# Float32 projections as four products of 32 columns each, in a decoder layer on one core

## The chip, the core and the metric

The kernel runs on one core of a Trainium2 chip. The metric is the time of one execution on the device in microseconds. The core has five engines with their own instruction streams: TensorE (PE in the profile, its weight loads PEld), VectorE (DVE), ScalarE (ACT), GpSimd (POOL) and SyncE (SP, which here only issues DMAs). TensorE is an array of 128 rows by 128 columns. The rows carry the contraction, the columns the output partitions. A product (a matmul instruction of the kernel) first loads its stationary operand into the array and then streams its moving operand past it; results go to PSUM, which the kernel uses in banks of 128 partitions by 512 float32. A product that is less than 128 rows tall or less than 128 columns wide takes only a strip of the array, and products on different strips can run side by side.

## What is computed

One decoder layer on `x` of 128 sequences by 128 tokens by 256 features, in float32: self attention, cross attention with a context of the same shape, and a feed-forward block with ternary weights, each with a layer norm ahead of it and a residual sum behind it. Cut to what matters here:

```python
def attention(q_in, kv_in, Wq, Wk, Wv, Wo, mask):       # 16 heads of 16 features
    Q, K, V = q_in @ Wq.T + bq, kv_in @ Wk.T + bk, kv_in @ Wv.T + bv
    scores = einsum("bhqd,bhkd->bhqk", Q, K) / 4         # cross: where(mask == 0, 1e-9, scores)
    return einsum("bhqk,bhkd->bhqd", softmax(scores), V) @ Wo.T + bo
x = x + attention(layernorm(x), layernorm(x), ...)       # self
x = x + attention(layernorm(x), context, ..., mask)      # cross
h = layernorm(gelu(layernorm(x) @ ternary(W_fc).T)) * ln_w + ln_b
x = x + h @ ternary(W_proj).T
```

The eight products with `Wq`, `Wk`, `Wv` and `Wo` (four for each attention, all of 256 by 256 weights) are the projections that the change is about.

## The kernel before

**Tiling.** Work goes by groups of four sequences, 512 tokens, so there are 32 groups. Features lie on partitions in two chunks of 128 (`CC = 2`). A weight matrix is one tile `[128, 2, 256]` in float32.

**Streams and order.** The kernel is written as Python generators, one for each kind of work, and each `yield` ends a step. Stream A is the attention itself (`maxima`, `outputs`, `transposed_scores`, `transposed_maxima`, `weights`, one sequence at a time), n prepares self attention (`prepare_self`), k the keys and values of cross attention (`prepare_keys`), c ends self attention and makes the queries of cross attention (`prepare_cross`), f ends cross attention and does the feed-forward block (`finish`). Three strings of letters, `START`, `ORDER` (112 letters, run 28 times) and `END`, say which stream does its next step. Each engine executes its instructions in exactly that order, so on TensorE a projection step can stand behind a step of any other stream.

**The projections.** `product_halves` makes the transposed queries and keys (tiles `pq`, `pk`, line 317): for one half `o` of the output features it issues two products, one for each chunk `c` of the contraction, with a stationary block of 128 by 128 weights and a moving operand of 512 tokens. There is a step border between the two. `row_halves` makes values and output rows (`pv`, `po`, line 329): for two blocks of 128 tokens it issues two products each, with the 128 tokens stationary and 256 weight columns moving. All of them are products of the whole array, in float32. ScalarE takes `pq` and `pk` out of PSUM (lines 374 and 351), VectorE `pv` and `po` (lines 365 and 411).

**Shapes on TensorE.** In the profile a group's shape gives rows*columns of the array. Beside the projections these are there:

- whole array, 128*128: transposes `pt` (line 297), `pg` (470) and `pn` (718), and the feed-forward products `ph` (436) and `py` (494), these two with float32r operands;
- row strips, 32*128, four side by side: the scores `s` (691), the transposed scores `st` (749) and what is added to them (773);
- column strips, 128*32, four side by side: the attention outputs `av` (794), written as four products into partitions 0 to 31, 32 to 63, 64 to 95 and 96 to 127 of one bank;
- 32*32, sixteen side by side: the mask products (680), in bfloat16.

A float32 product leaves two LDWEIGHTS and two MATMUL records in the trace; a transpose or a float32r product leaves one of each.

**Banks.** `bank(name)` gives one of three PSUM banks to each step of projections, transposes and feed-forward in turn (`BANKS = 3`); scores have two pairs of banks of their own, `av` and `pn` share one.

Of the kernel before, what the change touches and what calls it, by code (L numbers as in the profile page):

```python
# [27 lines left out]
P = 128  # L28
# [3 lines left out]
CC = D // P  # L32
# [5 lines left out]
S4 = 4  # L38
# [31 lines left out]
def tile_decoder_layer(ctx: ExitStack, tc: tile.TileContext, a: dict, out: bass.AP):  # L70
    nc = tc.nc
# [115 lines left out]
    def bank(name):  # L187
        return ps_mm.tile([P, 512], F32, name=name, tag="mm")
# [113 lines left out]
    def transposed_copy(x):  # L302
# [7 lines left out]
        yield from transposed(x, evacuate)  # L310
        return xn_t[0]

    def product_halves(w, o, src_t, name):

        out = bank(name)
        for c in range(CC):
            nc.tensor.matmul(  # L317
                out, w[:, c, o * P : (o + 1) * P], src_t[:, c], start=(c == 0), stop=(c == CC - 1)
            )
            if c == 0:  # L320
                yield
        return out

    def row_halves(w, src_t, j0, name):

        rows = bank(name).rearrange("p (j d) -> p j d", j=2)
        for j in range(2):
            for c in range(CC):
                nc.tensor.matmul(  # L329
                    rows[:, j],  # L330
                    src_t[:, c, (j0 + j) * P : (j0 + j + 1) * P],
                    w[:, c],
                    start=(c == 0),
                    stop=(c == CC - 1),
                )
            if j == 0:
                yield
        return rows
# [3 lines left out]
    def keys_values(w, src_t, unit):  # L342
        nonlocal n_values


        for o in range(CC):
            pk = yield from product_halves(w["k"], o, src_t, "pk")
            if o == 0:
                kt = unit["k"] = p_act.tile([P, CC, 2, T], F32, name="kt", tag="kt", bufs=3)
            for e in range(2):  # L350
                nc.scalar.activation(
                    kt[:, o, e],
                    pk,
                    AF.Identity,
                    bias=w["bk"][:, o, e : e + 1],
                    scale=parity[:, e : e + 1],
                )
            yield
        for j0 in range(0, G, 2):
            rows = yield from row_halves(w["v"], src_t, j0, "pv")  # L360
            if j0 == 0:
                v = unit["v"] = values[n_values % 3]
                n_values += 1
            heads = v[:, j0 : j0 + 2, 0 : H * VC].rearrange("p j (h d) -> p j h d", d=VC)
            nc.vector.tensor_copy(heads[:, :, :, 0:HD], rows.rearrange("p j (h d) -> p j h d", d=HD))  # L365
            if j0 == 0:
                yield

    def queries(w, xn_t, unit):
        for o in range(CC):  # L370
            pq = yield from product_halves(w["q"], o, xn_t, "pq")
            if o == 0:
                qt = unit["q"] = p_act.tile([P, CC, T], F32, name="qt", tag="qt", bufs=3)
            nc.scalar.activation(qt[:, o], pq, AF.Identity, bias=w["bq"][:, o : o + 1], scale=Q_SCALE)
            if o == 0:
                yield
# [15 lines left out]
    def projected(w, x, sums, o_raw):  # L392

        r = p_stat.tile([P, T // 8], F32, name="r", tag="r", bufs=2)
        nc.vector.reciprocal(r, sums)

        by_head = p_dram.tile([CC, 8, T], F32, name="by_head", tag="by_head")
        nc.sync.dma_start(by_head.rearrange("o h (j t) -> (o h j) t", j=8), r)
        factors = p_act.tile([P, CC, T], F32, name="factors", tag="factors", bufs=1)
        for o in range(CC):  # L400
            nc.sync.dma_start(factors[:, o], by_head[o][:, None, :].to_broadcast([8, HD, T]))
        yield

        for o in range(CC):
            for half in range(2):
                tok = slice(half * T // 2, (half + 1) * T // 2)
                nc.gpsimd.tensor_tensor(o_raw[:, o, tok], o_raw[:, o, tok], factors[:, o, tok], ALU.mult)  # L407
        yield
        for j0 in range(0, G, 2):
            rows = yield from row_halves(w["o"], o_raw, j0, "po")  # L410
            nc.vector.tensor_tensor(x[:, j0 : j0 + 2], x[:, j0 : j0 + 2], rows, ALU.add)
            yield
# [481 lines left out]
```

## Time and profile before

| | us |
|---|---|
| median of 3 runs | 2746.52 (2745.23 to 2748.5) |
| the profiled execution, its own time | 2749.66 |
| its span, first to last instruction | 2747.6 |
| LDWEIGHTS busy | 1953.2 (71%) |
| VectorE busy | 2051.7 (75%) |
| ScalarE busy | 1552.0 (56%) |
| GpSimd busy | 1367.6 (50%) |

TensorE's costliest groups, by line and shape. The columns are the line, engine and operation, output and inputs, rows*columns of the array, the moving operand, the number of records, their busy time (us) with what overlaps counted once, the mean time of one (ns), and the idle time ahead of them.

```profile
L691 PE MATMUL s<-kt,qt 32*128 32x256 f32 x4096 | 296.9, 401 | 1.6 <-ACT w_t L782 1.5
L794 PE MATMUL av<-w_t,v 128*32 128x128 f32 x8192 | 278.1, 276 | 4.4 <-DVE q_max L723 1.3
...
L329 PE MATMUL pv<-xattn_wv,ctx_t 128*128 128x256 f32 x512 | 134.4, 386 | 0.0
L317 PE MATMUL pk<-ctx_t,xattn_wk 128*128 128x512 f32 x256 | 134.1, 607 | 0.0
```

The mean time of one record is longer than the room it takes: [...] the next ones start meanwhile. Busy time divided by count is nearer to the room. The granted TensorE clock is 0.995 of full speed over the span. The DMA engines are busy about a fifth of the time.

### The profile page before, as it was taken

What the parts mean: (1) busy time and instruction counts of PE and PEld (TensorE: products, weight loads), DVE (VectorE), ACT (ScalarE), POOL (GpSimd) and SP (SyncE); (2) the same over time, 40 slices, a digit from 0 to 9 for tenths busy, and PEclk for the clock granted to TensorE, in tenths of its full rate; (3) what the DMA queues carried; (4) which work ended last, traced back from release to release, by engine and by line L of the source; (5) the groups of instructions that cost most, each with busy time, mean ns of one, the idle gap of its engine ahead of it and who ended that gap; (6) DMA issues with size and microseconds to landing.
All of it is one profiled execution on the core that took longest, in us unless ns stands there. A gap on an engine that the chain in (4) does not pass through costs nothing.

```text
span 2747.6 us, 76951 instructions
## 1 busy us (share of the span) xinstructions
PE 2698.6 (98%) x32845; PEld 1953.2 (71%) x32845; DVE 2051.7 (75%) x3793; ACT 1552.0 (56%) x2380; POOL 1367.6 (50%) x1427
## 2 busy tenths in 40 slices
PE   7999999999999999999999999999999999999998
PEld 4567777777777777777777777777777777777767
DVE  5777777777787777787777877777877777877677
ACT  3355565555655555655555655555665556655446
POOL 2355454545554545544554545454545455545334
PEclk9999999999999999999999999999999999999999
DMA  3121121221211211212211212211212212212210
GB/s 102 49 50 32 51 50 41 57 51 34 55 42 49 57 43 40 57 41 50 57 34 48 57 36 54 57 34 49 50 40 57 57 30 53 45 46 50 49 25 16
DMA packets 110044, 130.28 MB, mean 47 GB/s; under 512 B 32264, under 2 KB 69000, under 8 KB 109704
## 3 DMA queue, kind: packets, MB, share of 16 engines
q1 hardware_dynamic: 109704, 125.37, 19.0%
q8 instruction: 260, 4.26, 0.6%
q14 instruction: 80, 0.66, 0.1%
HBM read 71.38 MB, written 18.84 MB: 33 GB/s over the span
## 4 chain that ended last, share of the span: by engine, by line
PE 94%; DVE 3%; POOL 1%; issue 1%; ACT 1%; DMA 1%; SPq 0%; ACTq 0%; DVEq 0%; POOLq 0%
PE st L749 10%; PE s L691 10%; PE av L794 9%; PE py L494 9%; PE ph L436 9%; PE po L329 9%; PE pq L317 8%; PE pv L329 8%; PE pk L317 8%; PE pg L470 4%; PE pt L297 3%; PE st L773 3%; PE s L680 2%; PE pn L718 1%; DVE mx L702 1%
## 5 line engine op out<-in xcount | busy, mean ns | idle before, releaser
L702 DVE TENSOR_REDUCE mx<-s 128x8 f32<-128x1024 f32 x512 | 600.6, 1215 | 66.5 <-PE s L691 64.3
L782 ACT ACTIVATE w_t<-st 128x1024 f32<-128x1024 f32 x512 | 496.7, 1023 | 194.2 <-PE st L749 166.3
L274 POOL TENSOR_SCALAR rstd<-agg 128x4 f32<-128x4 f32 (+2 forms) x163 | 40.0, 246 | 1099.8 <-DVE agg L269 1094.3
L279 POOL TENSOR_SCALAR xn<-x,agg,rstd 128x256 f32<-128x256 f32 x380 | 460.6, 1225 | 9.9
L759 DVE COPY_PREDICATED_SCALAR st<-masked_t,masked_score 128x1024 f32 x256 | 315.6, 1278 | 63.3 <-PE st L749 60.1
L479 ACT ACTIVATE g<-pg,ln_w 128x256 fp32r<-128x256 f32 (+1 forms) x520 | 212.5, 475 | 203.9 <-PE pg L470 188.7
L797 ACT COPY raw<-av 128x512 f32<-128x512 f32 x256 | 150.2, 587 | 302.6 <-PE av L794 301.8
L691 PE MATMUL s<-kt,qt 32*128 32x256 f32 x4096 | 296.9, 401 | 1.6 <-ACT w_t L782 1.5
L407 POOL TENSOR_TENSOR o_raw<-o_raw,factors 128x256 f32<-128x256 f32 x252 | 176.4, 728 | 232.0 <-DMA factors<-by_head 177.0
L794 PEld LDWEIGHTS av<-w_t,v 128*32 128x32 f32 x8192 | 210.0, 110 | 112.1 <-issue 29.9
L794 PE MATMUL av<-w_t,v 128*32 128x128 f32 x8192 | 278.1, 276 | 4.4 <-DVE q_max L723 1.3
L436 PE MATMUL ph<-w_fc,xn 128*128 128x512 f32 x1024 | 273.2, 409 | 1.4 <-DVE g L481 1.4
L279 POOL TENSOR_SCALAR g<-g,agg,rstd 128x1024 f32<-128x1024 f32 x63 | 271.0, 4301 | 6.6
L494 PE MATMUL py<-w_proj,g 128*128 128x256 f32 x2048 | 268.6, 285 | 0.6 <-DVE g L481 0.6
L494 PEld LDWEIGHTS py<-w_proj,g 128*128 128x128 f32 x2048 | 250.7, 190 | 15.6 <-issue 11.1
L691 PEld LDWEIGHTS s<-kt,qt 32*128 32x128 f32 x4096 | 186.9, 184 | 104.5 <-issue 57.8
L481 DVE SCALAR_TENSOR_TENSOR g<-pg,ln_w,g 128x256 fp32r<-128x256 f32 (+1 forms) x520 | 217.3, 472 | 28.5 <-ACT g L479 26.6
L436 PEld LDWEIGHTS ph<-w_fc,xn 128*128 128x128 f32 x1024 | 187.1, 190 | 54.3 <-DVE g L279 9.3
L723 DVE SCALAR_TENSOR_TENSOR q_max<-pn,max_rows,qt 128x256 f32<-128x256 f32 x256 | 110.6, 474 | 101.5 <-PE pn L718 101.4
L443 ACT ACTIVATE g<-ph 128x512 f32<-128x512 f32 x256 | 146.3, 596 | 70.5 <-PE ph L436 69.8
L365 DVE COPY v<-pv 128x512 f32<-128x512 f32 x128 | 86.2, 674 | 123.6 <-PE pv L329 123.5
L268 DVE BATCH_NORM_STATS2 stats<-g 128x6 f32<-128x512 f32 x256 | 162.4, 679 | 0.9 <-ACT g L443 0.8
(128 smaller groups left out, 4679.1 us busy)
## 6 DMA issues: line engine op xcount, KB each, us to landing
o_raw<-raw SPq DMA_DIRECT2D x504, 64.0 KB
factors<-by_head SPq DMA_DIRECT2D x126, 256.0 KB
x<-in_x_dram SPq DMA_DIRECT2D x32, 512.0 KB
ctx_t<-in_ctx_t_dram SPq DMA_DIRECT2D x32, 512.0 KB
out_dram<-x SPq DMA_DIRECT2D x31, 512.0 KB
sums<-raw SPq DMA_DIRECT2D x126, 16.0 KB
by_head<-r SPq DMA_DIRECT2D x63, 32.0 KB
raw_w<-in_w_fc_t_dram SPq DMA_DIRECT2D x1, 1024.0 KB
```

Source lines behind the costliest of these rows:

```text
L279: engine.tensor_scalar(dst[:, j], src[:, j], agg[:, j, 0:1], rstd[:, j : j + 1], ALU.subtract, ALU.mult)
L317: nc.tensor.matmul(out, w[:, c, o * P : (o + 1) * P], src_t[:, c], start=(c == 0), stop=(c == CC - 1))
L329: nc.tensor.matmul(rows[:, j], src_t[:, c, (j0 + j) * P : (j0 + j + 1) * P], w[:, c], start=(c == 0), stop=(c == CC - 1),)
L436: nc.tensor.matmul(ph, xn_parts[i][:, c, (j0 + j - at) * P : (j0 + j - at + 1) * P], w_fc[:, c, n * 512 : (n + 1) * 512], start=((i, c) == ...
L481: nc.vector.scalar_tensor_tensor(parts[1][:, f0 + f, tok], pieces[:, f], scales[f], parts[0][:, f0 + f, tok].bitcast(F32), ALU.mult, ALU.s ...
L494: nc.tensor.matmul(rows[:, j], parts[i][:, f, j * P : (j + 1) * P], w_proj[:, f], start=((i, f) == terms[0]), stop=((i, f) == terms[-1]),)
L691: nc.tensor.matmul(s[r // 2][:, r % 2, 2 * o : 2 * o + 2], qt[strip, o, tok], kt[strip, o, :, tok], start=(stage == "self"), stop=True, sk ...
L702: nc.vector.tensor_reduce(mx[:, 2 * half : 2 * half + 2], s[half], AX.X, ALU.max, negate=True)
L749: nc.tensor.matmul(s[r // 2][:, r % 2, n], kt[strip, n // 2, n % 2, tok], added[strip, n // 2, n % 2] if stage == "self" else qt[strip, n ...
L759: nc.vector.copy_predicated(s[half].rearrange("p r n q -> p (r n) q"), masked_t[:, None, :].to_broadcast([P, 8, P]), masked_score[:, :, No ...
L782: nc.scalar.activation(w_t[:, 2 * half : 2 * half + 2], s[half], AF.Exp)
L794: nc.tensor.matmul(av[32 * r : 32 * r + 32, n], v[:, j, head : head + 32], w_t[:, r, n], start=True, stop=True)
```

## The change

Each product in `product_halves` and `row_halves` becomes four. A new helper, `in_strips`, cuts the stationary operand into four blocks of 32 columns and issues a product for each, with the same moving operand, into the 32 partitions of the output that belong to these columns. The four write the same PSUM bank that the one product wrote, with the same start and stop flags, and the sums are the same. What is around the two functions stays: the strings of letters, the step borders, the banks, the readers of the banks, and every other product, also the few projections that `finish_rows` issues itself for the last group (line 634).

```diff
+    def in_strips(out, stationary, moving, c):
+        for r in range(S4):
+            strip = slice(r * 32, (r + 1) * 32)
+            nc.tensor.matmul(
+                out[strip],
+                stationary[:, strip],
+                moving,
+                start=(c == 0),
+                stop=(c == CC - 1),
+                skip_group_check=True,
+            )
+
     def product_halves(w, o, src_t, name):
         out = bank(name)
         for c in range(CC):
-            nc.tensor.matmul(
-                out, w[:, c, o * P : (o + 1) * P], src_t[:, c], start=(c == 0), stop=(c == CC - 1)
-            )
+            in_strips(out, w[:, c, o * P : (o + 1) * P], src_t[:, c], c)
             if c == 0:
                 yield
@@
         for j in range(2):
             for c in range(CC):
-                nc.tensor.matmul(
-                    rows[:, j],
-                    src_t[:, c, (j0 + j) * P : (j0 + j + 1) * P],
-                    w[:, c],
-                    start=(c == 0),
-                    stop=(c == CC - 1),
-                )
+                in_strips(rows[:, j], src_t[:, c, (j0 + j) * P : (j0 + j + 1) * P], w[:, c], c)
             if j == 0:
                 yield
```

In the built program the order of the instructions on all engines is the same as before, but for each projection product standing four times.

## The prediction, made before the changed kernel ran

> **What bounds the kernel now.** I read the page first: the busy shares, then the chain of work that ended last.
>
> ```profile
> PE 2698.6 (98%) x32845; PEld 1953.2 (71%) x32845; DVE 2051.7 (75%) x3793; ACT 1552.0 (56%) x2380; POOL 1367.6 (50%) x1427
> ...
> PE 94%; DVE 3%; POOL 1%; issue 1%; ACT 1%; DMA 1%; SPq 0%; ACTq 0%; DVEq 0%; POOLq 0%
> ```
>
> TensorE is busy 98% of the span and makes up 94% of the chain; no other engine is above 75%. Next, whether a stretch in the middle differs, by the busy times of 700 to 2100 us (columns: length, then PE, PEld, DVE, ACT, POOL busy, clock, DMA):
>
> ```profile
> 700.00:2100.00 1400.00, 1398.14 (x17265) 1014.60 (x17264) 1061.35 (x1959) 810.87 (x1245) 725.77 (x746) 1.00 0.20 47
> ```
>
> 1398 of 1400 us: here TensorE waits for nobody, at full clock. What it waits for in all, by the list of waits, is 14.8 us between 60 and 2650 us (the longest group is `pt` for GpSimd's `xn`, 4.6 us), 10.3 us in the last 98 us, and the rest in the first 60 us. So a microsecond more or less on TensorE is a microsecond of the kernel, less what these few waits absorb.
>
> What TensorE does with its time is best seen in the chain in order of time (start, length, engine, tile, line, records):
>
> ```profile
> 1306.38 0.60 PE st L773 x15
> 1306.97 1.05 PE pk L317 x2
> 1308.03 0.44 PE pg L470 x4
> 1308.47 0.86 PE pk L317 x2
> 1309.33 1.08 PE s L691 x16
> 1310.40 1.01 PE av L794 x32
> 1311.41 0.59 PE pg L470 x4
> 1312.00 0.87 PE pv L329 x4
> 1312.87 0.44 PE pg L470 x4
> 1313.30 0.86 PE pv L329 x4
> 1314.17 1.10 PE st L749 x32
> ...
> 1315.53 1.89 PE py L494 x16
> 1317.42 0.87 PE pt L297 x8
> 1318.29 1.07 PE s L691 x16
> 1319.37 2.08 PE py L494 x16
> 1321.44 1.01 PE av L794 x32
> ```
>
> The pieces touch, so each length is what the block costs. The same block has two prices. `pk` x2 costs 0.86 us behind `pg`, which has its shape (128*128), and 1.05 behind `st`, a row strip. `pg` x4 costs 0.44 behind `pk` and 0.59 behind `av`. `py` x16 costs 1.89 behind `pn` and 2.08 behind `s`. **A block pays an entry whenever the block before it has another shape of the array**, and the transposes, the float32r products and the float32 products of the whole array are one shape, since `pg` to `pv`, `pv` to `pg` and `pn` to `py` pay none. The entries by what is entered:
>
> - whole-array float32 (`pk`, and likewise `pv`, `pq`, `po`): 1.05 - 0.86, about **0.20 us** (1.06 in most other places);
> - transposes: 0.59 - 0.44 = **0.15**;
> - float32r: 2.08 - 1.89 = 0.19, I take **0.20**;
> - row strips: in the trace the quartets of `st` start 0.112 us apart and those of `s` 0.216, so 8 x 0.112 = 0.90 of the 1.10, and 4 x 0.216 = 0.86 of the 1.08: **0.21**, the same behind `pv` and behind `av` (1.10 in both);
> - column strips: the quartets of `av` start 0.109 us apart, 8 x 0.109 = 0.87 of the 1.01: **0.14**, the same behind `s` and behind `py`.
>
> **The change, part by part.**
>
> *The products themselves.* A quartet of strips streams the same 512 or 256 columns as the one product did. Records of the whole array take 0.430 us (`pk`, 0.86/2) and 0.216 (`pv`, 0.86/4). For quartets the near row is `av`, float32 in column strips: 0.109 us at 128 columns, half of `pv`'s 0.216 at 256. `s`, in row strips, takes 0.216 at 256, equal to `pv`. So 0 for each of the 3056 quartets (1024 of line 317, 2032 of line 329), which is 1024 x 0.430 + 2032 x 0.216 = 879 us before and after.
>
> Two rules of the Trainium skill speak against that 0. "TensorE: Matmul & The Clock Gate", section "Measured speedup vs the span model", has products side by side last one product's time plus 4 ns for each further one, and three column strips measured at 2.38 times one instead of 3. Taken for every quartet, the first would be 3 x 4 ns x 3056 = +37 us, the second 879 x (3/2.38 - 1) = +229 us. The row decides: the strips of `av`'s first quartet do start 6 to 7 ns apart, but the next quartet follows after 0.109 us all the same, so the stagger is paid once and lies inside the 0.14. These are the upper ends; the lower end is 0, as the columns to stream don't get fewer.
>
> *Weight loads.* 128 columns take 190 ns, 32 columns 110 ns (the mean of `av`'s loads), four at a time. Inside a run both lie under the products, of 216 ns at least, so nothing is gained there; on entry it is the exposed load that makes 0.14 of 0.20.
>
> *More instructions.* 3 x 3056 = 9168 products and as many loads more. `av` passes 64 records in 1.01 us; quartets at 256 columns need 32 in 0.86. Issue isn't the limit: 0. If it were, `av` would show it.
>
> *The entries.* This is where the change costs. I counted what stands on either side of each unbroken run of projection steps in TensorE's instruction order, which is fixed: 628 runs. Ahead of them: row strips 290, transposes 270, `av` 36, float32r 30, unchanged float32 products 2. Behind them: transposes 272, row strips 219, `av` 65, the 32*32 mask products 37, float32r 31, unchanged float32 products 4. With the prices above:
>
> - before, runs behind row strips and behind `av` paid 0.20: (290 + 36) x 0.20 = -65.2 us, gone;
> - now all but those behind `av` enter column strips: (628 - 36) x 0.14 = +82.9;
> - `av` behind a run no longer enters: 65 x 0.14 = -9.1;
> - transposes, float32r and unchanged products behind a run now enter: 272 x 0.15 + 31 x 0.20 + 4 x 0.20 = +47.8;
> - row strips and mask products behind a run paid before and pay now: 0.
>
> Sum **+56.4 us**. In one view: a run between two row-strip blocks would gain 0.06, but of the commonest kinds, 214 stand between row strips and transposes (-0.06 + 0.15), 151 between transposes and row strips (+0.14), 57 between transposes on both sides (+0.29).
>
> *What lies beside.* ScalarE and VectorE read the banks when the last strip is done, later by the entries only; with 25% and more idle they are no new bound. Of TensorE's 25 us of waits after the start a few fit under the added time; I take 3 us. So 2749.7 + 56.4 - 3 = 2803 us against the profiled execution. The median of the runs lay 3.1 us under that execution, so **2800 us**.
>
> **The rivals.**
>
> 1. *Entries to and from transposes are cheap, and it gets faster.* If a column strip behind a transpose, or a transpose behind it, cost nothing, the (270 + 30) x 0.14 + 272 x 0.15 + 31 x 0.20 = 89 us would go and -33 stay: 2717 against the profile, 2714 by the median. It decides if these 603 entries cost under 33/603 = 0.054 us on average in place of 0.148. For it: only six places in the trace have `av` behind a transpose. Against: in these six the first quartet comes 0.09 us late and the second 0.025 late, as behind `pq` and `py`, and `pg` behind `av` is the 0.59 above, at 57 places. Chance 0.04.
> 2. *Each quartet pays its stagger*, 12 ns by the rule above: 2800 + 37 = 2837. For it: quartets of 512 columns are not in the trace. Against: `av` and `s`. Chance 0.08.
> 3. *The strips don't run fully abreast with long streams*: +229, 3029. Chance 0.03.
> 4. *The change is hidden or undone*: the entries fall where TensorE would have waited. Against: 25 us of waits for 56 of entries, none of them between 700 and 2100 us to speak of. Within 0.2% chance 0.02.
>
> **How the numbers follow.** The forecast has 0.83. Its own range: all waits after the start absorbed (-22) at one end, entries 0.02 us dearer at some 900 places (+18) at the other, so 2778 to 2818; as waits go only where an entry happens to precede them, I put the low end at 2784. Half of rival 2 takes the high end to 2826. A measurement of this kernel can tell about 0.2%, 5.5 us, from no change. Faster than that: rival 1 and a rest, 0.05. Within: 0.02. Slower: 0.93.
>
> **What would show it.** In the profile after, chain pieces of projections with the strips' records: 0.86 us for a step of one 512-column product or two of 256 behind `av`, 1.00 behind anything else, never 1.06. `pg` x4 at 0.59 behind a projection in place of 0.44. `st` and `s` unchanged at 1.10 and 1.08, `av` 0.87 behind a projection. TensorE still about 98% busy, its waits no longer than before. Wrong, if projection quartets start more than 0.22 or 0.435 us apart, or if `pg` stays at 0.44.

## The result, and the profile after

| | us |
|---|---|
| median before (4 runs) | 2745.88 |
| median of the changed kernel (4 runs) | 2796.36 |
| ratio | 1.0178, 95% interval 1.0166 to 1.0189 |
| the profiled execution, its span | 2797.67, 2795.7 |
| predicted | 2800, range 2784 to 2826 |

The change makes the kernel 1.8% slower: +50.5 us by the medians, +48.1 by the spans of the two profiled executions. The page after, busy times and the chain that ended last by engine:

```profile
PE 2747.2 (98%) x42013; PEld 1760.7 (63%) x42013; DVE 2052.0 (73%) x3793; ACT 1550.7 (55%) x2380; POOL 1368.1 (49%) x1427
...
PE 94%; DVE 2%; DMA 1%; POOL 1%; ACT 1%; issue 1%; SPq 0%; ACTq 0%; DVEq 0%; POOLq 0%
```

TensorE is busy 48.6 us longer, with 9168 more records (4584 more products, two records each), and stays the engine that sets the end. The others do what they did (DVE 2052.0 us against 2051.7). Weight loads were busy 192.5 us less, and the kernel is not faster for it: inside a run of projections they lie under products. From the busy times by stretch, with the columns of the same view before:

```profile
700.00:1400.00 700.00, 700.00 (x10829) 448.08 (x10825) 519.57 (x953) 404.72 (x618) 352.89 (x364) 1.00 0.20 49
```

TensorE is full here at full clock, so what it does with the time is again read from the chain in order of time (start, length, engine, tile, line, records). It is the same stretch of the order as the one shown of before, some 26 us later, as much as the change had cost by then:

```profile
1332.10 0.44 PE pg L476 x4
1332.53 0.11 PE pn L724
1332.64 0.60 PE st L779 x15
1333.24 0.99 PE pk L318 x8
1334.23 0.59 PE pg L476 x4
1334.82 0.99 PE pk L318 x8
1335.82 1.08 PE s L697 x16
1336.89 1.01 PE av L800 x32
1337.90 0.59 PE pg L476 x4
1338.49 1.00 PE pv L318 x16
1339.49 0.59 PE pg L476 x4
1340.08 1.00 PE pv L318 x16
1341.08 1.10 PE st L755 x32
...
1355.56 0.99 PE pq L318 x8
1356.55 0.87 PE av L800 x32
...
1362.95 1.07 PE av L800 x32
1364.02 1.73 PE po L318 x32
```

`pk` behind the row strips of `st` went from 1.05 to 0.99 us, behind `pg` from 0.86 to 0.99. `pg` between projections went from 0.44 to 0.59. `pv` between transposes went from 0.86 to 1.00. `s` and `st` kept 1.08 and 1.10. Two things got cheaper: `av` behind `pq` costs 0.87 in place of 1.01, and `po` behind `av` 1.73 (two steps) in place of 1.92. The kernel before, at these two places:

```profile
1328.54 0.86 PE pq L317 x2
1329.40 1.01 PE av L794 x32
...
1335.96 1.08 PE av L794 x32
1337.04 1.92 PE po L329 x8
```

The gains are at few places (36 runs behind `av`, 65 ahead of it), the losses at many (270 runs have a transpose ahead of them, 272 one behind).

### The profile page after: what moved, and what is told of

Read it like the earlier page. It is cut to its first block, busy times and chain, and to the rows that moved or that the text cites. A ratio compares the mean times of both kernels' runs of the same rounds, so it can differ in the third digit from the quotient of the medians.

```text
span 2795.7 us, 95374 instructions
## 1 busy us (share of the span) xinstructions
PE 2747.2 (98%) x42013; PEld 1760.7 (63%) x42013; DVE 2052.0 (73%) x3793; ACT 1550.7 (55%) x2380; POOL 1368.1 (49%) x1427
## 4 chain that ended last, share of the span: by engine, by line
PE 94%; DVE 2%; DMA 1%; POOL 1%; ACT 1%; issue 1%; SPq 0%; ACTq 0%; DVEq 0%; POOLq 0%
PE st L755 10%; PE s L697 10%; PE ph L442 9%; PE py L500 9%; PE av L800 9%; PE pk L318 8%; PE pv L318 8%; PE po L318 8%; PE pq L318 8%; PE pg L476 5%; PE pt L297 3%; PE st L779 3%; PE pn L724 2%; PE s L686 2%; DVE mx L708 1%
## 5 line engine op out<-in xcount | busy, mean ns | idle before, releaser
L800 PEld LDWEIGHTS av<-w_t,v 128*32 128x32 f32 x8192 | 216.2, 110 | 97.7 <-issue 80.3
L476 PEld LDWEIGHTS pg<-ident,g 128*128 128x128 f32 x1024 | 109.3, 140 | 93.6 <-issue 51.9
```

The source lines that it names most:

```text
L476: nc.tensor.transpose(pieces[:, f, j * P : (j + 1) * P], g[:, j, (f0 + f) * P : (f0 + f + 1) * P], ident,)
L800: nc.tensor.matmul(av[32 * r : 32 * r + 32, n], v[:, j, head : head + 32], w_t[:, r, n], start=True, stop=True)
```

## The experiments

Three theories stood against each other. **Entry**: a block pays when the block before it on TensorE has another shape of the array; all of the +50 us comes from the borders of the projection runs. **Price per quartet**: four products side by side cost a little more than one, whatever stands around them. **Price per product**: it goes by the number of instructions. Counts are of TensorE's instruction order; an entry price is what a block costs over the time of its quartets or products, as a median over the traces of before and after: 0.196 us into a whole float32 product, 0.136 into column strips, 0.151 into a transpose, about 0.2 into the rest. The edits below are cut to what matters; but for that of `ORDER` they are made in the changed kernel.

**One kind of projection alone.** In `halves_only`, `row_halves` is as before; in `rows_only`, `product_halves` is.

```diff
 # halves_only: only queries and keys in strips
-                in_strips(rows[:, j], src_t[:, c, ...], w[:, c], c)
+                nc.tensor.matmul(rows[:, j], src_t[:, c, ...], w[:, c], start=(c == 0), stop=(c == CC - 1))
 # rows_only: only values and output rows in strips
-            in_strips(out, w[:, c, o * P : (o + 1) * P], src_t[:, c], c)
+            nc.tensor.matmul(out, w[:, c, o * P : (o + 1) * P], src_t[:, c], start=(c == 0), stop=(c == CC - 1))
```

> Only queries and keys (512 columns moving) in strips, values and output rows whole. Entry theory: what costs are the changes of array shape around a run of projection steps, and queries/keys and values/rows now break each other's runs too. Counted in TensorE's order with the entry prices of the trace: +48 us, less the tenth by which the full change came out below its count: +43, so about 2789, nearly the whole of the change's +50. Rival, a price for each quartet of strips: 1024 of 3056 quartets, a third of +50, +17 (or +25 if it goes by columns streamed): 2763 to 2771.

> Only values and output rows (256 columns moving) in strips. Entry theory: counted +44 us, less a tenth +40: about 2786; together with halves_only far more than the change itself, because entries between the two kinds are paid in each of these and not in the full change. Rival, a price for each quartet: +33 (or +25 by columns): 2771 to 2779, and the two must add up to +50.

Measured: 2785.08 and 2779.98 us beside 2747.35 before; ratios 1.0134 (1.0119 to 1.0148) and 1.0115 (1.0099 to 1.0131), so +37.7 and +32.6. They were expected at +43 and +40, so both are some 5 to 8 us under what the entry theory expected. But the two halves of the change cost 70 us one by one and 50 together. Prices per quartet or per product would add up to 50; borders between the two kinds, which are paid in each half and not in the whole, make the excess. The chain in order of time has such a place, first in `halves_only`, then in the changed kernel:

```profile
1351.41 1.06 PE pv L341 x4
1352.47 0.99 PE pq L318 x8
1353.46 1.06 PE pv L341 x4
```

```profile
1358.53 1.00 PE pv L318 x16
1359.53 0.86 PE pq L318 x8
1360.39 0.86 PE pv L318 x16
```

`halves_only` pays three entries there, the change one. By the count the excess would be 32 us, and 20 came: waits, `py` and the first and last groups take some 11 us from each half alone and 7.8 from the whole change.

**Another width.** Two products of 64 columns in place of four of 32.

```diff
-        for r in range(S4):
-            strip = slice(r * 32, (r + 1) * 32)
+        for r in range(2):
+            strip = slice(r * 64, (r + 1) * 64)
```

> Two products of 64 columns in place of four of 32, all projections. Entry theory: 128*64 is one more shape, so the same entries come in at a price between 0.14 and 0.20 us and runs next to the attention outputs (128*32), free in the change, now pay as well: +60 to +80 us, 2806 to 2826, slower than four of 32. If one entry of 64 is no shape change against 32, it is at +50 or below. Rival, a price by the number of extra products (one where the change has three): a third of +50, 2763.

Measured: 2809.06 us beside 2747.35, ratio 1.022 (1.0205 to 1.0234), +61.7, at the low end of the expected +60 to +80. A third of the extra products costs more, which ends the price per product. The chain of this kernel in order of time shows why:

```profile
1366.43 1.05 PE av L800 x32
1367.48 1.88 PE po L318 x16
1369.36 1.10 PE st L755 x32
...
1374.90 1.87 PE pq L318 x8
1376.77 1.01 PE av L800 x32
```

`po` behind `av` pays 0.15 again (1.88 against 1.73) and `av` behind `pq` 0.14 (1.01 against 0.87): 64 columns next to 32 is a change of shape too, and the few places that the change had made cheaper are lost. Counted with 0.149 us into strips of 64 the cost would be +78. By the spans 20 us of that are missing: some 12 are waits in the middle groups that shrank and 4 are `py`, both as told below for the change; most of the rest lies in the first and last groups.

**A change of shape inside every run.** Of the two products that are summed into one output, the first in strips, the second whole. This halves the number of quartets and multiplies the borders.

```diff
     def in_strips(out, stationary, moving, c):
+        if c == CC - 1:
+            nc.tensor.matmul(out, stationary, moving, start=False, stop=True, skip_group_check=True)
+            return
         for r in range(S4):
```

> Of the two products that are summed into one output, the first in strips and the second of the whole array, in all projections: half the quartets of the change, but a change of shape inside every run. Entry theory: counted with 0.136 us into strips and 0.196 us into a whole float32 product +166 us, less up to 10 us that falls into waits: 2902 to 2912. Rival, a price for each quartet: half of +50, 2772.

Measured: 2907.6 us beside 2748.86, ratio 1.0576 (1.056 to 1.0592), +158.7, inside the expected 2902 to 2912. The chain in order of time:

```profile
1403.13 0.99 PE pq L321 x8
1404.13 1.06 PE pq L317 x2
1405.19 1.00 PE pq L321 x8
```

Each piece is one product of 512 columns, eight records in strips or two whole, and each pays its entry: 0.99 and 1.00 in strips (line 321), 1.06 whole (line 317), where 0.86 is the price without. Half the quartets cost three times as much as all of them, which ends the price per quartet.

**The same quartets, fewer borders.** Twelve letters of `ORDER` are changed so that steps of one stream stand together between attention steps, once in the kernel before as a control (`grouped_before`) and once in the changed kernel (`grouped_after`).

```diff
-    "cfknAAfkfknAAfccnAfAfAcccAAnncAAknkAAfAffAffnffAAnnAAnnAnAffcnAAffAAffnAffnfffcAfkfAfAnnfcAAcffkfkAA"
+    "cfknAAffkknAAfccnAfAfAcccAAnncAAkknAAfAffAffffnAAnnAAnnAnAffcnAAffAAffnAfffffncAffkAfAnnfcAAcfffkkAA"
     "ffcccAfffAAk"
```

> Whole-array projections; 12 letters of the steady order changed so that steps of the same stream stand together (kfkf becomes kkff and so on). Entry theory and rival alike: counted shape changes as before (+0.2 us), so 2746, unless the new order itself makes TensorE wait for a bank; it is the control for the next run.

> The change (all projections in strips) with the same 12 letters changed. Entry theory: fewer borders between projections and transposes, counted 16 us less than the change, so +40 by count against its own control, less a tenth +36, and some 14 to 16 us below the changed kernel: about 2781. Rival, a price for each quartet: the number of quartets is the same, so 2796 plus what the control shows.

Measured, both beside 2749.62 us of the kernel before: the control 2750.47 (ratio 1.0008, 1.0001 to 1.0015), the change in this order 2778.34 (1.0111, 1.0096 to 1.0126). So the change costs 27.9 us in this order (expected 36) and 50.5 in the other, with the same products in both. The fall of 23 us is larger than the 16 counted. Nearly all of the rest lies at one place of each group, where the new order puts two steps of `pk` behind two of `pg`. The chain in order of time has it in the control and then with the change:

```profile
1377.81 0.87 PE pg L470 x8
1378.68 1.95 PE pk L317 x4
```

```profile
1391.48 1.02 PE pg L476 x8
1392.51 1.85 PE pk L318 x16
```

In the control `pk` has the shape of `pg` and no entry to pay, yet takes 1.95 us in place of 1.72 (4 x 0.430). By the turn of the three banks it writes the bank that held `po`, and its first load waits for VectorE's reading of it (line 411, until 1378.60). The timeline has in brackets how long the loads stood idle and what ended that:

```profile
1378.65 0.30 PEld L317 LDWEIGHTS pk<-ctx_t,xattn_wk 128*128 128x128 f32 x2 [0.21 <-DVE x L411]
```

With the change `pk` pays its entry of 0.14 and loses nothing to that wait. It takes 0.10 less than in the control in place of the 0.14 more that was counted, which is 6.7 us at 28 places.

**Strips only where they should gain.** A string of flags, one for each of the 1528 projection products in order, chooses strips or the whole array; `in_strips` reads the next flag. In `strips_where_free` the flags are set for runs with no whole-array block on either side, in `strips_behind_outputs` only for those directly behind `av`.

```diff
     def in_strips(out, stationary, moving, c):
+        if next(strips_of) == "0":
+            nc.tensor.matmul(out, stationary, moving, start=(c == 0), stop=(c == CC - 1), skip_group_check=True)
+            return
         for r in range(S4):
```

> Strips only for the 235 of 1528 projection products whose runs stand between blocks none of which has the whole array's shape (attention outputs, row strips, mask products), whole products elsewhere. Entry theory: runs beside the attention outputs lose an entry, runs between row strips get the cheaper one: counted -15 us, so 2731 to 2735, faster than before. Rival, a price for each quartet: 235/1528 of +50, +8 us, 2754.

Measured: 2740.57 us beside 2747.35, ratio 0.9977 (0.9966 to 0.9987). It is faster than both kernels, where a price per quartet would make it slower; but the gain is 6.8 us and not the 15 counted. In the trace the time from one group's output sum to the next, averaged over 24 groups in the middle, fell from 83.07 to 82.87 us, by 0.20 where 0.39 were counted. The chain in order of time shows where the rest went, first before, then in this kernel:

```profile
1344.40 1.91 PE pq L317 x4
1346.31 1.01 PE av L794 x32
1347.33 1.24 PE st L749 x30
```

```profile
1341.57 1.85 PE pq L333 x16
1343.42 0.87 PE av L815 x32
1344.30 1.44 PE st L770 x32
```

`pq` and `av` gave the counted 0.06 and 0.14; `st` behind them grew from 1.24 to 1.44 and took both back. Its scores go into the PSUM tiles that VectorE must first have reduced. The timeline of this kernel (start, length, engine, line, operation) has that reduction:

```profile
1342.17 2.35 DVE L723 TENSOR_REDUCE mx<-s 128x8 f32<-128x1024 f32 x2
```

It ends at 1344.52, and the first products of `st` into the second of the two tiles start at 1344.57. Before, it ended at 1347.35, these products started at 1347.41, the same 0.05 behind, and `st` was already late by 0.14 there (1.24 against the usual 1.10). A shorter way from `s` to `st` ends in this wait. That reading was tested by leaving the run ahead of `av` whole again:

> Strips only for the 138 projection products whose run stands directly behind the attention outputs; the runs directly ahead of the attention outputs, in strips in strips_where_free, are whole again. If the gain missing there (counted 0.39 us for each group, steady period shorter by 0.20) is spent by the transposed scores, which come up earlier and then wait for VectorE behind the run ahead of the attention outputs, then leaving that run whole costs nothing: steady period 82.87 us as there, time 2740 to 2742. If entries are simply worth half of what was counted, the period is shorter than before by 0.10 only, 82.97, time 2744.

Measured: the group's time is 82.87 us, the same as with the other run in strips; 2742.58 us beside 2748.86, ratio 0.9978 (0.9968 to 0.9987). The expected 2740 to 2742 was for a kernel before at 2747; the difference of 6.3 us agrees. The run ahead of `av` is worth nothing here, the run behind it all of the 0.20 (counted 0.196).

## Why the prediction was right

The forecast stood 53.5 us above the median that it started from; 50.5 were measured.

**That TensorE sets the end** held: 98% busy and 94% of the chain, before and after.

**The products themselves at 0** held. Quartets of 512 columns start 0.429 us apart and those of 256 columns 0.216, the same as whole products. So neither the stagger (+37 us) nor the measured 2.38 (+229 us), which the prediction took from the Trainium skill ("TensorE: Matmul & The Clock Gate", section "Measured speedup vs the span model"), is paid for each quartet of this stream; rivals 2 and 3 are out by the trace alone.

**Weight loads and instructions at 0** held: loads were busy 192.5 us less, there are 9168 more records of products (the prediction calls them products) and as many of loads, and the pieces inside runs kept 0.86.

**The entries** carried the sum, and their place and sign held term by term. The prices were rounded up a little: column strips were entered at 0.136, not 0.14, whole products at 0.196, not 0.20. With these the count is -63.9 + 80.5 - 8.8 + 41.1 + 7.0 = +55.9 in place of +56.4. That the exposed load makes the price of an entry, as the prediction has it, no run tests by itself; the last section has what speaks for it.

**What lies beside** was the term that was mis-sized: the prediction took 3 us, and the step from the counted 55.9 to the 48.1 of the spans is 7.8. In the pieces of one group, some 4.8 us over 30 groups are waits that shrank: `s` of the mask products, 0.57 before and 0.44 after (0.36 without a wait), `s` behind it 1.15 and 1.08 with 0.04 of idle time that is gone, while `st` behind `av` grew from 1.24 to 1.32. The first of them, before and after:

```profile
1353.07 0.86 PE pk L317 x2
1353.93 0.57 PE s L680 x16
```

```profile
1380.05 0.99 PE pk L318 x8
1381.04 0.44 PE s L686 x16
```

The two together take 1.43 us in both: what `pk` adds, the wait behind it loses. The list of waits that the prediction read holds idle time and could not show this: the wait is some 0.21 us (0.57 against 0.36), and a record of the mask products lasts 0.38, so the one before still counts as busy. So rival 4, entries that fall where TensorE would have waited, was right in kind for 4.8 of the 56 us. About 1.9 us more come from `py`, which the change does not touch (last section). The remaining microsecond is in the first and last groups and is not assigned.

**The range** held the result, but its high end of 2826 does not follow from the sums given for it: half of rival 2's 37 us on top of 2818 is 2836.

**Rival 1**, cheap entries beside transposes, fell with `pg` at 0.59 and `pk` behind `pg` at 0.99. The strips gained where no whole-array block was the neighbour, and there half of the count was lost to VectorE's reduction.

## What to carry to other kernels

Splitting a full-width product into column strips saved nothing in the stream itself here; what it changed is the shape of the array, so ask which shape stands before and behind, and count these borders in TensorE's order rather than the products. Give neighbours the same shape, or group steps of one shape together, before changing the shape of one of them. Price each border from a block that occurs in the trace behind both kinds of neighbour, and look for a wait just behind a block that gets shorter or longer: in the chain it shows as a block that takes longer than the same block elsewhere, and not always as idle time.

## What the runs showed of the hardware that was not expected

The entry goes by what is entered and hardly by what is left or by how long the products are: 0.136 us into column strips of 32 at 128, 256 and 512 moving columns, 0.149 into strips of 64, 0.196 into whole float32 products, with medians from 0.134 to 0.140, 0.147 to 0.150 and 0.194 to 0.197 over what stood before and over the kernels. Strips of 32 and of 64 columns count as two shapes.

The entries rise with the mean time of one weight load in these traces: 110 ns for strips of 32 columns, 136 for strips of 64, 141 for a transpose and 190 for a whole float32 product go with entries of 0.136, 0.149, 0.151 and 0.196 us. On entry the first load starts together with the record of its product (`pk` before, both at 1306.90), inside the run 0.43 us ahead of it (1307.01 and 1307.44). Both fit an exposed load as the larger part of the price; no run changed a load alone.

Products that no experiment touches ran at two speeds. A `py` block of 32 float32r products directly behind `st` started them 0.118 us apart in every steady group before; in the changed kernel 13 of 28 such blocks ran at 0.113, at the same full clock. With strips of 64 all 28 were fast, in `rows_only` and in the grouped change 18, in `halves_only` and `alternating` none. The mean spacing of `py`, gaps over 0.2 us left out, was 0.1178 us before, 0.1168 after, 0.1158 with strips of 64 and 0.1164 in the grouped change; over 2048 products that is 1.9 to 4.1 us less. Why it happens stays open.
